# Attention over neighbours, then order statistics of neighbours: the search for neighbours in seven blocks instead of six, and seven edits to what waits for what

## The chip, the cores and the metric

The kernel runs on one core of a Trainium2 chip. The metric is the device time of the whole program in microseconds (us), the median over several runs; lower is better. The engines are named as in the profile: PE (matrix), PEld (its weight loads), DVE (vector), ACT (scalar), POOL (general, here the issuer of indirect DMAs) and SP (here the issuer of plain DMAs).

## What is computed

Inputs are 4096 nodes of 128 features and a 4096 x 4096 adjacency matrix of integers, some 64 neighbours in a row and at most 100. Layer 0 is graph attention with eight heads, layer 1 takes quantiles over neighbours. Cut to what matters:

```python
# layer 0
Wh = einsum('nd,hde->hne', nodes, W)
e = leaky_relu(f1[:, :, None] + f2[:, None, :], 0.2)       # f1, f2 from Wh, a1, a2
att = softmax(where(adj > 0, e, -9e15), axis=-1)
h = elu(einsum('hnm,hmd->hnd', att, Wh))
x = layernorm(nodes + elu(cat_of_heads(h) @ W1 + b1)) * gamma + beta
# layer 1
rank = cumsum(adj != 0, axis=1) - 1
keep = mask & ~((rank + 1) % skip == 0)                    # skip: about half the count of neighbours
svals = sort(where(keep, x, big), axis=neighbours)         # each feature by itself
agg = sum over q in (0.25, 0.5, 0.75) of svals[ceil(q * n_keep) - 1] / 3
out = (0.5 * agg + 0.5 * x) @ W.T + b + x
```

## The kernel before

The kernel is written for a framework that records instructions in program order and then orders each engine's queue itself: among the instructions that its own timing model holds ready it takes the one recorded first. The order on an engine is thus fixed when the program is built, by that model's times. `tc.issue_after(ins)` keeps what is recorded inside it behind `ins` on the same engine; `tc.declare_no_dep(a, b)` takes away a dependency that the framework would otherwise keep by a semaphore.

**Search.** The nodes are 32 tiles of 128 rows. `Front` finds each row's neighbours: SP loads the adjacency in quarters of a tile (L378), ACT turns them to 0 and 1 (L380, L387), PE packs 16 columns into a word (L389), and DVE draws the non-empty words and then the columns out of the words by rounds of eight maxima (`first`, `second` and a last drain, L188 and L190). Tiles are grouped into blocks, `BLOCKS = (4, 4, 6, 6, 6, 6)`, and inside a block the rows are ordered by their count of neighbours: `place` computes each row's place (`pos_i`, L518), and POOL writes its list there by an indirect DMA (L541 into `rows_d`). Since the rows are ordered, each group of 16 rows has a bound on its count of neighbours that holds for any likely input; `BOUNDS[n]` lists it for a block of n tiles, and a flag sends other inputs to a general path. `keep` writes what layer 1 needs (`meta_d`), and at the end `order` computes each row's place among all 4096 rows, which 32 indirect DMAs write into `order_d` (L680, `late` in `gat`).

`Front.pieces` cuts this work into a list: for each block, one `first` per tile, a `second` for up to four tiles together, a last drain per tile, `place`, and `keep` of the block before. `gat` draws from the list: `EARLY` = 5 pieces ahead of the loop, two after each half tile (`advance(2)`), and `through(b)` until block b is placed where its lists are needed.

**Attention.** `gat` goes over 64 half tiles u, each 64 rows. `load(u)` has POOL gather the neighbours' rows of `xf_d` (L971, 128 rows by one DMA, into buffers `nb`) and, once a tile, the tile's own rows (`me`, L947); it runs three half tiles ahead. Ahead of a block's first gathers SP loads the lists back (L903, L919, L932). `probabilities` has DVE and ACT form the logits and the softmax (L1054 to L1088), starting from `mine` (L989), which needs `me`; `rows_sum` spreads the weights over rows (DVE, L1103) and PE sums the products (L1111). `combine` takes two tiles at a time, in stages drawn one per half tile from the list `going`, through the heads' matrices and the layer norm (to L1194), and POOL writes the rows to their nodes' places in `x1_d` (L1197, in the profile `x_d<-s`).

**Sort.** `sparse` goes over 32 tiles of the globally ordered rows. `load(t)` has POOL gather the tile's `info` (L1867), its own rows `xs`, and 50 to 100 neighbours a row (L1713) from `x1_d` into one of three buffers `rows`. A network of comparators then sorts the neighbours of all 128 rows and 128 features at once. A step compares up to 16 pairs of columns: ACT copies the lower ones aside (L1751), to one of two PSUM tiles `low` or, up to four pairs, to SBUF (`low_s`), and DVE writes minimum (L1756) and maximum (L1757). `plan` splits a tile's network into a first part and the final merge; the second part of tile t-1 and the first part of tile t are interleaved. The steps of tile 0's first part take 8 pairs instead of 16. `quantile` and `pick` find the quantiles: ACT scales the candidates by weights of zero or one (L1810), PE sums them (L1815, L1818), and every four tiles `finish` applies the last layer on PE (L1835 to L1837), which ACT copies out (L1841) and POOL stores (L1845). This work waits in a list, `waiting`, and is put between the comparator's instructions: each step draws at most one entry, and PE's products go to the last 512 columns of a PSUM tile whose first columns a step of at most 12 pairs uses.

The sort begins with its own loads of `order` and a count `iota_p`, inside the branch that is taken once the flag has been read.

Of the kernel before, what the change touches and what calls it, by code (L numbers as in the profile page):

```python
# [50 lines left out]
P = 128  # L51
# [19 lines left out]
C3 = 8  # L71
# [21 lines left out]
MOST = 16  # L93
# [4 lines left out]
BLOCKS = (4, 4, 6, 6, 6, 6)  # L98
# [13 lines left out]
BOUNDS = {  # L112
    4: (
# [203 lines left out]

class Front:
# [88 lines left out]
    def second(self, t, m, k1, cand):  # L407

        nc, one = self.nc, self.one
        k1, cand = k1[:, :m], cand[:, :m]  # L410
        sp = self.spill[:, t : t + m, :]
        wf, base = decode(nc, one, k1, f"1_{m}")
        rest = one.tile([P, m, C1], F32, name=f"rest1_{m}")
        peel(nc, one, wf, base, cand[:, :, :C1], rest, f"1_{m}")
# [5 lines left out]
        k2 = one.tile([P, m, C2], F32, name=f"k2_{m}")  # L420
# [5 lines left out]
        wf, base = decode(nc, one, k2, f"2_{m}")  # L426
        rest = one.tile([P, m, C2], F32, name=f"rest2_{m}")
        peel(nc, one, wf, base, cand[:, :, C1 : C1 + C2], rest, f"2_{m}")
        nc.vector.tensor_scalar(base, base, 127.0 * NG1, None, op0=ALU.add)
        nc.vector.scalar_tensor_tensor(rest, rest, float(NG1), base, op0=ALU.mult, op1=ALU.add)  # L430
        k3 = one.tile([P, m, C3], F32, name=f"k3_{m}")
# [5 lines left out]
        wf, base = decode(nc, one, k3, f"3_{m}")  # L437
        for r in range(PEELS):
            nxt = one.tile([P, m, C3], F32, name=f"rest3_{m}", bufs=2)
            at = C1 + C2 + C3 * r  # L440
            peel(nc, one, wf, base, cand[:, :, at : at + C3], nxt, f"3_{m}")
            wf = nxt
        left = one.tile([P, m], F32, name=f"left_{m}")
# [353 lines left out]
def gat(tc, nc, c, x, adj, xf_d, meta_d, order_d, flag_d, w, a1, a2, w1, b1, gamma, beta, x1_d):  # L797
# [25 lines left out]
    with ExitStack() as ctx:  # L823
# [307 lines left out]
        def combine(t, zT):  # L1131
# [64 lines left out]
            for j in range(TWO):  # L1196
                nc.gpsimd.indirect_dma_start(  # L1197
# [4 lines left out]
                )  # L1202

        held = {u: load(u) for u in range(3)}
# [5 lines left out]
        for u in range(2 * NT):  # L1210
# [3 lines left out]
            elif late:  # L1214

                advance(len(todo))
                for piece in late:
                    piece()
                late = []
# [3 lines left out]
            if u + 1 < 2 * NT:  # L1223
                with ExitStack() as order:
                    for ins in behind:
                        order.enter_context(tc.issue_after(ins))
                    e, behind = probabilities(u + 1, held[u + 1], f1s[(u + 1) // 2])
            with ExitStack() as order:
                for ins in behind:
                    order.enter_context(tc.issue_after(ins))  # L1230
# [7 lines left out]
            advance(2)  # L1238
        for stages in going:
            for _ in stages:  # L1240
                pass
        advance(len(todo))
# [415 lines left out]
def plan(t):  # L1658
# [8 lines left out]
    first = steps(layers[:-merge], lambda i: i, PAIRS if t else PAIRS // 2)  # L1667
# [7 lines left out]
def sparse(tc, nc, c, x1_d, meta_d, order_d, w, b, out):  # L1675


    with tc.tile_pool(name="sp1", bufs=1) as one, tc.tile_pool(
# [15 lines left out]
        it = one.tile([P, 2 * MIDDLE], I32, name="it_p")  # L1694
# [612 lines left out]
```

## Time and profile before

| | |
|---|---|
| median of 3 runs | 8430.65 us (8417.16 to 8433.30) |
| profiled execution | 7646.96 us, of which the span is 7645.2 us |
| busy in the span | DVE 5831.7, POOL 4343.5, ACT 2214.1, PE 1122.8, PEld 946.8 us |
| gathers of the attention (L971) | 2190, 953 ns each, from 142.5 to 3106.6 us |
| gathers of the sort (L1713 `rows`) | 2078, 971 ns each, from 3170.6 to 7265.4 us |
| comparators (L1756, L1757, large steps) | 1022 each, 1862 and 1861 ns |
| POOL waiting for rows buffers (`rows` on ACT `picked`) | 1270.8 us in 28 waits |
| DVE waiting for gathers (L1054 on `nb`) | 1206.7 us in 115 waits |

The profiled execution is one of its own and took less time than the runs of the median, so a sum made from the profile is compared with the profiled time. A group of instructions has its busy time, its mean and the idle time of its engine just before it, with what ended that idle time. In a timeline a row gives start and length, the instruction, and in brackets the idle time before it and its releaser.

### The profile page before, as it was taken

Reading aid. Unit: us, or ns where it says so; the run is one execution under the profiler, and the core shown is the slowest. Engines: PE = TensorE matmul, PEld = TensorE weight load, DVE = VectorE, ACT = ScalarE, POOL = GpSimd, SP = SyncE. Lnnn points to the kernel's source line nnn. Section 1 sums busy time; section 2 is a strip of 40 time slices with the busy share of each in tenths; the row PEclk is TensorE's granted clock in tenths of the full one; section 3 lists DMA queues with packets and bytes.
Section 4 is the critical chain, followed back from the end, with each engine's and each line's share of the span. In section 5 each row is a group of like instructions: output and inputs, shape, how many; then the busy total and the mean of one; then the engine's idle time right before and its main releaser. Section 6 shows DMA issues by size and latency. Waiting matters only on the chain. (4 is left out here: it accounts for less than half of the span.)

```text
span 7645.2 us, 31290 instructions
## 1 busy us (share of the span) xinstructions
PE 1122.8 (15%) x6047; PEld 946.8 (12%) x6047; DVE 5831.7 (76%) x9380; ACT 2214.1 (29%) x2301; POOL 4343.5 (57%) x4524
## 2 busy tenths in 40 slices
PE   3243333322222322100000000000000000000001
PEld 1232222222222222100000000000000000000000
DVE  8465555565223222399999999999999999999999
ACT  6020212100000000144344343434334433443433
POOL 2777677777777777565554645455536434554500
PEclk5566666666566666655555555555555555555555
DMA  6242324222222222111111111111101101111100
GB/s 205 57 121 56 107 62 121 60 55 56 47 56 56 56 56 56 40 44 34 40 35 30 41 31 37 30 36 34 38 23 41 34 24 33 36 35 29 33 1 1
DMA packets 219057, 380.95 MB, mean 50 GB/s; under 512 B 129283, under 2 KB 129412, under 8 KB 218852
## 3 DMA queue, kind: packets, MB, share of 16 engines
q0 software_dynamic: 145808, 308.58, 15.3%
q1 hardware_dynamic: 72898, 70.23, 3.1%
q14 instruction: 156, 1.28, 0.1%
q8 instruction: 49, 0.80, 0.0%
q10 hardware_dynamic: 146, 0.07, 0.0%
HBM read 368.26 MB, written 10.31 MB: 50 GB/s over the span
## 5 line engine op out<-in xcount | busy, mean ns | idle before, releaser
L1713 POOL DMA_INDIRECT rows<-x_d,info x2078 | 2018.2, 971 | 1949.5 <-ACT picked L1810 1270.8
L971 POOL DMA_INDIRECT nb<-xf_d,ids x2190 | 2086.0, 953 | 707.0 <-issue 632.2
L1751 ACT COPY low<-rows 128x2048 f32<-128x2048 f32 (+8 forms) x1022 | 1561.5, 1533 | 2429.9 <-DVE rows L1757 1780.7
L1756 DVE TENSOR_TENSOR rows<-low,rows 128x2048 f32<-128x2048 f32 (+9 forms) x1022 | 1884.7, 1862 | 138.9 <-ACT low L1751 50.0
L1757 DVE TENSOR_TENSOR rows<-low,rows 128x2048 f32<-128x2048 f32 (+9 forms) x1022 | 1882.4, 1861 | 5.8
L1054 DVE TENSOR_TENSOR e<-nb,ps_small 128x64 f32<-128x64 f32 (+9 forms) x200 | 47.7, 240 | 1252.6 <-DMA nb<-xf_d,ids 1206.7
L1111 PE MATMUL ps_z<-spread,nb 128*128 128x128 f32 x4500 | 615.7, 305 | 797.9 <-DVE spread L1103 775.6
L1111 PEld LDWEIGHTS ps_z<-spread,nb 128*128 128x128 f32 x4500 | 604.5, 220 | 829.9 <-DVE spread L1103 420.7
L1815 PE MATMUL low<-sixth_i,picked 128*128 128x128 f32 x300 | 79.8, 442 | 4224.7 <-ACT low L1751 3736.4
L1815 PEld LDWEIGHTS low<-sixth_i,picked 128*128 128x128 f32 x300 | 66.8, 324 | 4237.7 <-ACT low L1751 3744.8
L1073 ACT ACTIVATE ps_e<-e 128x256 f32<-128x256 f32 (+4 forms) x64 | 26.1, 408 | 1936.2 <-DVE e L1054 972.6
L1103 DVE TENSOR_TENSOR spread<-e,ps_small 128x1152 f32<-128x1152 f32 (+4 forms) x312 | 342.7, 1107 | 129.2 <-PE ps_z L1111 79.4
L1845 POOL DMA_INDIRECT out<-o,info x32 | 34.4, 1076 | 392.9 <-ACT o L1841 369.2
L380 ACT ACTIVATE nz<-a_i 128x1024 bf16<-128x1024 int32 x128 | 134.3, 1051 | 292.5 <-DMA a_i<-in_adj 254.3
L1751 ACT COPY low_s<-rows 128x512 f32<-128x512 f32 (+3 forms) x325 | 139.8, 471 | 130.5 <-DVE rows L1756 48.0
L389 PE MATMUL ps_words<-nz,pows 128*128 128x512 bf16 (+1 forms) x272 | 113.7, 577 | 364.4 <-ACT nz L387 258.0
L188 DVE MAX8 k<-key 128x8 f32<-128x256 f32 x416 | 164.6, 412 | 0.7
L1756 DVE TENSOR_TENSOR rows<-low_s,rows 128x512 f32<-128x512 f32 (+3 forms) x325 | 158.3, 500 | 3.0 <-ACT low_s L1751 2.1
L1757 DVE TENSOR_TENSOR rows<-low_s,rows 128x512 f32<-128x512 f32 (+3 forms) x325 | 158.7, 500 | 0.3
L190 DVE MATCH_REPLACE8 key<-k,key 128x256 f32<-128x256 f32 x384 | 155.5, 407 | 0.0
L1142 PE MATMUL ps_h<-zT,w_ga 128*128 128x256 f32 x256 | 116.3, 619 | 198.4 <-DVE s L1414 106.6
L1759 DVE TENSOR_TENSOR rows<-rows 128x256 f32<-128x256 f32 (+8 forms) x245 | 141.6, 580 | 0.2
(246 smaller groups left out, 2528.0 us busy)
## 6 DMA issues: line engine op xcount, KB each, us to landing
a_i<-in_adj SPq DMA_DIRECT2D x128, 512.0 KB
nb<-xf_d,ids POOLq DMA_INDIRECT x2190, 2.5
rows<-x_d,info POOLq DMA_INDIRECT x2078, 2.5
xf_d<-xf POOLq DMA_DIRECT2D x4, 576.0 KB, 7.4
xf<-in_x POOLq DMA_DIRECT2D x4, 512.0 KB
meta_d<-rowdata_k SPq DMA_DIRECT2D x4, 324.0 KB
abc_ta<-in_L_gnn_a POOLq DMA_DIRECT2D x2, 512.0 KB, 7.7
w_ga<-in_L_gnn_W POOLq DMA_DIRECT2D x2, 512.0 KB
```

Source lines behind the costliest of these rows:

```text
L188: nc.vector.max(out=top, in_=work)
L190: nc.vector.match_replace(out=work, in_to_replace=top, in_values=work, imm_value=gone)
L380: nc.scalar.activation(nz[:, j, :], a_i, AF.Relu, scale=-1.0, accum_out=self.negative[:, k : k + 1],)
L971: gather = nc.gpsimd.indirect_dma_start(out=rows[:, used + i, :], out_offset=None, in_=xf_d, in_offset=bass.IndirectOffsetOnAxis(ap=ids[:, ...
L1103: last = nc.vector.tensor_tensor(spread[:, :m], e[:, at : at + m, :].unsqueeze(2).to_broadcast(shape), own.unsqueeze(1).unsqueeze(3).to_br ...
L1111: product = nc.tensor.matmul(ps_z[:, g, :], rows[:, k, :D], spread[:, i].rearrange("p j h -> p (j h)"), start=i0 + i == 0, stop=i0 + i == ...
L1713: nc.gpsimd.indirect_dma_start(out=row, out_offset=None, in_=x1_d, in_offset=bass.IndirectOffsetOnAxis(ap=info[:, col : col + 1], axis=0),)
L1751: nc.scalar.copy(packed, lows)
L1756: nc.vector.tensor_tensor(lows, packed, highs, op=ALU.min)
L1757: nc.vector.tensor_tensor(highs, packed, highs, op=ALU.max)
L1759: nc.vector.tensor_tensor(lows, lows, highs, op=ALU.min)
L1815: nc.tensor.matmul(made["ps"], made["v"][:, i, :], sixth, start=i == 0, stop=False)
```

## The change

The blocks become 2, 4, 4, 6, 6, 6 and 4 tiles, with a table of bounds for two tiles, and in the first 20 half tiles three pieces of the search are drawn instead of two. To this come the edits of what waits for what:

- the stores into `x1_d` no longer depend on each other;
- the 32 writes of the order are kept behind the last half tile's gathers on POOL;
- `order` and the `info` of tiles 0 and 1 are loaded in `gat`, ahead of the last `combine`, and `iota_p` is made at the start;
- minimum and maximum of a step no longer depend on products in other columns of the PSUM tile;
- the scalings of a pick are drawn one at a time;
- a tile's own rows are gathered after its neighbours, and a tile's `info` and gathers are kept behind the gathers of the tile before;
- tile 0's first part takes steps of 4 pairs.

The temporary tiles of `second` are shared between counts of tiles (names without the count, all of `BATCH` size), and `picked` holds 14 rows instead of 16. Cut to these, the diff is:

```diff
-MOST = 16
+MOST = 14
-BLOCKS = (4, 4, 6, 6, 6, 6)
+BLOCKS = (2, 4, 4, 6, 6, 6, 4)
 BOUNDS = {
+    2: (54, 58, 58, 60, 62, 62, 64, 66, 66, 68, 70, 70, 72, 76, 78, 100),
...
+class Batches:
+    def __init__(self, pool):
+        self.pool = pool
+    def tile(self, shape, dtype, name, **kw):
+        full = [shape[0], BATCH, *shape[2:]]
+        return self.pool.tile(full, dtype, name=name, **kw)[:, : shape[1]]
...
     def second(self, t, m, k1, cand):
-        nc, one = self.nc, self.one
+        nc, one = self.nc, Batches(self.one)
...
 def gat(...):
             for j in range(TWO):
-                nc.gpsimd.indirect_dma_start(
+                done = nc.gpsimd.indirect_dma_start(
                     out=x1_d,
...
+                for other in stored:
+                    tc.declare_no_dep(done.ins, other, reason="each node has a row of its own")
+                stored.append(done.ins)
...
                 advance(len(todo))
-                for piece in late:
-                    piece()
+                with tc.issue_after(gathers[2 * NT - 1][HALF - 1, 0]):
+                    for piece in late:
+                        piece()
...
-            advance(2)
-        for stages in going:
+            advance(3 if u < 2 * START[3] else 2)
+        for stages in going[:-1]:
             for _ in stages:
                 pass
-        advance(len(todo))
+        for i in range(4):
+            nc.sync.dma_start(
+                out=order[:, ts(i, NT // 4)],
+                in_=order_d[ts(i, N // 4), :].rearrange("(t p) c -> p (t c)", p=P),
+            )
+        for t, info in enumerate(infos):
+            nc.gpsimd.indirect_dma_start(
+                out=info,
+                out_offset=None,
+                in_=meta_d,
+                in_offset=bass.IndirectOffsetOnAxis(ap=order[:, t : t + 1], axis=0),
+            )
+        for stages in going[-1:]:
+            for _ in stages:
+                pass
...
 def plan(t):
-    first = steps(layers[:-merge], lambda i: i, PAIRS if t else PAIRS // 2)
+    first = steps(layers[:-merge], lambda i: i, PAIRS if t else PAIRS // 4)
...
 def compare(rows, step):
                 nc.scalar.copy(packed, lows)
+                aside = []
                 if waiting and waiting[0][0] == "copy":
                     waiting.pop(0)[1]()
                 elif waiting and SMALL < k <= PAIRS - FOUR:
-                    waiting.pop(0)[1](t[:, (PAIRS - FOUR) * D :])
-                nc.vector.tensor_tensor(lows, packed, highs, op=ALU.min)
-                nc.vector.tensor_tensor(highs, packed, highs, op=ALU.max)
+                    aside = waiting.pop(0)[1](t[:, (PAIRS - FOUR) * D :])
+                for to, op in ((lows, ALU.min), (highs, ALU.max)):
+                    done = nc.vector.tensor_tensor(to, packed, highs, op=op)
+                    for product in aside:
+                        tc.declare_no_dep(done.ins, product, reason="other columns of the bank")
...
 def pick(found, x1, comT):
-            def scale():
-                made["v"] = tp.tile([P, MOST, D], F32, name="picked", bufs=1)
-                for i, (v, weight) in enumerate(found):
-                    nc.scalar.mul(made["v"][:, i, :], v, weight)
+            def scale(i):
+                if i == 0:
+                    made["v"] = tp.tile([P, MOST, D], F32, name="picked", bufs=1)
+                nc.scalar.mul(made["v"][:, i, :], *found[i])
...
-            return [
-                ("copy", scale),
+            return [("copy", lambda i=i: scale(i)) for i in range(len(found))] + [
                 ("bank", sums),
...
 def load(t):
-            info = three.tile([P, MW], I32, name="info", bufs=3 * FOUR)
-            group[first][2].append(info)
-            nc.gpsimd.indirect_dma_start(
-                out=info,
-                out_offset=None,
-                in_=meta_d,
-                in_offset=bass.IndirectOffsetOnAxis(ap=order[:, t : t + 1], axis=0),
-            )
-            gather(group[first][0][:, t - first, :], info, NODE)
-            for s in range(HIGH[t]):
-                gather(rows[:, s, :], info, s)
+            with ExitStack() as after:
+                if gathered:
+                    after.enter_context(tc.issue_after(gathered[-1]))
+                if t < len(infos):
+                    info = infos[t]
+                else:
+                    info = three.tile([P, MW], I32, name="info", bufs=2 * FOUR + 2)
+                    nc.gpsimd.indirect_dma_start(
+                        out=info,
+                        out_offset=None,
+                        in_=meta_d,
+                        in_offset=bass.IndirectOffsetOnAxis(ap=order[:, t : t + 1], axis=0),
+                    )
+                group[first][2].append(info)
+                for s in range(HIGH[t]):
+                    done = gather(rows[:, s, :], info, s)
+                gather(group[first][0][:, t - first, :], info, NODE)
+                gathered.append(done.ins)
```

## The prediction

> **What bounds the kernel now.** I read the busy slices first, then windows, then the timeline of single engines at the places where one stage hands over to the next. The page's slices show two stages with different limits:
>
> ```profile
> PE   3243333322222322100000000000000000000001
> ...
> DVE  8465555565223222399999999999999999999999
> ...
> POOL 2777677777777777565554645455536434554500
> ```
>
> A slice is 191 us. Up to slice 17 POOL is the steady engine (the attention layer); from there DVE stands at 9 (the sorting layer). Two windows (sums for PE, PEld, DVE, ACT, POOL, then clock and DMA) say the same in numbers:
>
> ```profile
> 2400.00:2600.00 200.00, 45.23 (x277) 41.91 (x276) 51.15 (x136) 11.44 (x21) 150.82 (x160) 0.60 0.24 56
> ...
> 4500.00:5500.00 1000.00, 35.33 (x126) 28.79 (x126) 967.43 (x628) 396.11 (x303) 533.86 (x540) 0.50 0.12 35
> ```
>
> In the first, 160 indirect DMAs in 200 us are 1.25 us each: 0.95 of work and 0.30 of "issue" before each. POOL is full, though it shows 75%. In the second DVE is idle 33 us in 1000. So the attention layer ends when POOL's queue is empty, and the sort when DVE's is. POOL's timeline at the start (start, length, instruction, idle before and its releaser):
>
> ```profile
> 133.25 1.04 POOL L541 DMA_INDIRECT rows_d<-rowdata,pos_i  x1 [57.96 <-DVE pos_i L518]
> ...
> 142.51 0.99 POOL L971 DMA_INDIRECT nb<-xf_d,ids  x1 [4.40 <-DMA ids<-rows_d]
> ```
>
> POOL waits 58 us for DVE to find and place the neighbours of the first block, and the first gather goes out at 142.5. From there to 3106.6 POOL runs 2314 instructions, about 2900 us at 1.253, and waits about 64. Among them, by the view of the tile, are the order's writes:
>
> ```profile
> L680 POOL DMA_INDIRECT order_d<-node,pos_g x32: 954/958/991, 1920.5 to 2026.1; - x32
> ```
>
> They sit between gathers, in the middle of the full queue. At its end POOL stands still:
>
> ```profile
> 3105.62 0.94 POOL L971 DMA_INDIRECT nb<-xf_d,ids  x1 [0.30 <-issue]
> 3146.65 0.98 POOL L1197 DMA_INDIRECT x_d<-s,info  x1 [40.09 <-DVE s L1194]
> ...
> 3162.97 0.99 POOL L1867 DMA_INDIRECT info<-meta_d,order  x1 [0.72 <-issue]
> ...
> 3170.57 0.94 POOL L1713 DMA_INDIRECT rows<-x_d,info  x1 [0.30 <-issue]
> ```
>
> It idles 40 us for the last layer norms, and the sort's first row is fetched 64 us after the last gather. In the sort, DVE's waits from 3240 us on (total, times, longest):
>
> ```profile
> DVE rows L1756 <- ACT low L1751: 46.5, 48, 1.9
> DVE rows L1756 <- PE low L1837: 20.3, 8, 3.3
> DVE rows L1756 <- PE low L1818: 12.3, 10, 2.2
> ```
>
> DVE waits 33 us for matmuls whose products it does not read. Their surroundings, once:
>
> ```profile
> 5761.84 2.29 DVE L1756 TENSOR_TENSOR rows<-low,rows 128x2048 f32<-128x2048 f32 x1 [1.94 <-ACT low L1751]
> 5766.58 1.23 DVE L1756 TENSOR_TENSOR rows<-low,rows 128x1024 f32<-128x1024 f32 x1 [2.45 <-PE low L1837]
> ```
>
> [...] 128x768 takes 0.96 us and 128x1024 1.22, which leaves 0.18 at no columns.
>
> **The change part by part**, against the profiled 7645.2 us.
>
> *Two tiles first.* The maxima of tiles 0 and 1 are done at 45.1 us in DVE's timeline; for four tiles `second` ran 79.8 to 95.1 (15), the last drains to 123 (7.0 a tile), `place` to 133 (10). For two I take 11, 14 and 9: 79 us. The pad memsets, which waited until 70.6, may hold DVE on the way: plus 4. From `pos_i` to the first gather it was 9.6 us with four scatters, 7 with two. First gather at 90: **-52** (-45 to -60). The counts of the two bound tables give 2196 gathers instead of 2190: +7.5. Two more of the 32 neighbour scatters fall after the first gather: +2.5.
>
> *Does the second block come in time?* Its gathers are due after 141 gathers and two `me`, 179 us after the first: at 269. Before, DVE was held at `mine` of tile 1 until 77 us after the first gather, since that row comes in turn. Now that is near 171; behind it stand four drains (28), `place` (10) and two half tiles' logits and spreads (22): 231, then 10 to the gathers. It is in time by 28 us, and POOL still pays the landing chain that cost 4.4 at the first block: +5 (0 to 80, the upper end if `place` stands behind half tile 3's logits on DVE). The three later stalls on `info<-rows_d`, 12.3 us in five block edges, become six edges: +2.5.
>
> *Three pieces of search per half tile.* DVE spent 942 us in 200 to 1800, and 287 per 1000 where no search runs (2000 to 3000). A half tile's attention costs 0.287 x 44.9 = 13 us; what remains of the search is 582 us by my count for 30 tiles and 83 pieces, 7 a piece. Two pieces make 27 us, three 34, against 44.9 of gathers. Gathers cover it: 0. The cover is buffers for about two half tiles ahead; its failures cost 36.9 before (POOL on `ps_z`).
>
> *Order written last.* 32 x 1.256 = **-40.2** in the full queue. They now lie in the 40.09 us of idle after the last gather and end just when the first `x_d` store is ready: covered, to within 2 us. *Stores without waits for each other:* -10.6 in the queue (POOL on `x_d<-s`).
>
> Sum to the last gather: -52 + 7.5 + 2.5 + 5 + 2.5 - 40.2 - 10.6 = **-85**.
>
> *Hand-over.* Behind the last order write (+41 us after the last gather) SP loads the order (landing 3.6, four loads, 2 to land: +49), then POOL the two infos and the last two stores (ready at +48.3 as before): +54, landed +56.5. Rows start at +57 instead of +64: **-7** (-10 to +3, if SP's loads land late, since the last stores queue behind them). The iota and the `xs` gather leave the way too; they are in this number.
>
> *Finer steps for tile 0.* Between 3170.6 and 3236 DVE worked 21 us of 65. With 4-pair steps the first starts 10 us earlier and more fits; some 25 more steps cost 2 x 0.18 each, 9 us, in idle time. The next tile's rows arrive no earlier: **-6** (-12 to +5).
>
> *Products not waited for.* The 12.3 of L1818 go, less 1. The 20.3 of L1837 come with waits of 1.7 to 1.9 on ACT just before, five of them, because the matmul held the smaller step back (second line above): 29.7 together. But the products take 6 us, and the bank's next copy stands behind the copy of the products; I keep 13. Together **-24** (0 to -40).
>
> *Scaling one at a time.* The 46.5 us on ACT are mostly copies that start the moment DVE ends, data or bank, not bursts of scaling: 0 (-5 to +5). Rows buffers come free four steps later, some 13 us; POOL waited 15 us or more for all but one of them, and tile 31's landed about 30 us before its use. *Infos behind the gathers:* 2.4 us per tile in that same slack. The shared tiles and MOST change no instruction on a queue.
>
> Total -85 - 7 - 6 - 24 = **-122**: 7523 span, 7525 with the 1.8 around it. The median of the runs shown is 1.1025 times the profiled 7647.0; I see no reason in the profile and scale all: 8430.65 x 7525/7647 = **8296**.
>
> **Rivals.** *B, the gather queue starves:* the second block comes 50 us late or the denser search holds back the buffers. For it: 21.6 us at 883 and 8.5 at 820 already, with DVE at 66%. Against it: all 28 later scatters waited only for issue. The 52 are lost: -70, 8353. *C, new waits:* the bank's release takes the products' place and the order's loads land late: -31 gone, -91, 8330. *D, slower:* DVE becomes the bound of the first 20 half tiles. It decides from 122/20 = 6 us over the 44.9 a half tile, 51 against my 34; at 56 us it costs 220: +98, 8539. Against it: 17 us of room. *E, the order's writes do not move,* or land on the last stores' way: -82, 8340.
>
> **Chances.** All parts: 0.58, its own range 8245 to 8340. B 0.18, C 0.08, E 0.06, D 0.07, about level 0.03. Only D is slower; 0.2% is about what a measurement of this kernel can tell from no change. The best ends together give -160 (8254), and 8235 if gathers count for more outside the profile; the high end takes B and some of its excess. Range 8235 to 8375.
>
> **What would show it.** First gather near 90 and no POOL idle over 10 us near 270; L680 after the last L971; last gather near 3021; rows 57 us after it; no DVE wait on L1818 or L1837, and a small one on ACT in place of the latter. Wrong if POOL shows more than 100 us on `ps_z` or `pos_i`, or if DVE's idle time in the sort stays above 75 us.

## The result and the profile after

The changed kernel took 8584.31 us (median of 4 runs, 8568.83 to 8590.3), the kernel before beside it 8431.97 (8417.16 to 8437.66): ratio **1.0181, interval 1.0162 to 1.0199**. It is 152 us slower where 135 us less were forecast; 8584 lies far above the range.

The sign goes with the chip: on two chips (called here the **7650 chips**) the kernel before takes 7648 to 7651 us, on two others (the **8400 chips**) 8381 to 8426. One of the 8400 chips was used twice, more than two hours apart, with the 7650 chips in between, and gave 8426 and 8421; each other chip was used once. By its 7645 us the profile of before that the prediction read belongs to the first kind; the runs above, before and after, belong by their times to the second. On a 7650 chip the same changed kernel is faster, 7558.88 against 7647.76: ratio **0.9883, interval 0.9867 to 0.9900**.

The busy slices of the changed kernel as recorded, 215 us each:

```profile
PE   2213222223232323230000000000000000000000
...
DVE  4646466554222222234898979989899898998999
...
POOL 4454555566666666657255435536454535444410
```

Where POOL stood at 7 in the profile of before it stands at 4 to 6, and DVE in the sort drops from an even 9 to 8 in many slices. In windows (sums for PE, PEld, DVE, ACT, POOL, then clock and DMA):

```profile
2400.00:2600.00 200.00, 53.70 (x251) 46.04 (x250) 45.61 (x120) 9.44 (x18) 136.61 (x145) 0.58 0.20 51
...
4500.00:5500.00 1000.00, 35.32 (x126) 28.79 (x126) 921.59 (x691) 377.09 (x311) 481.56 (x503) 0.50 0.12 33
```

POOL issues 145 DMAs in the first window against 160, and DVE idles 78 us in the second against 33. Neither queue is full. The times of single steps, by POOL's timeline (start, length, instruction, idle before and its releaser), at the first block:

```profile
93.20 1.04 POOL L553 DMA_INDIRECT rows_d<-rowdata,pos_i  x1 [16.32 <-DVE pos_i L530]
...
101.30 0.98 POOL L985 DMA_INDIRECT nb<-xf_d,ids  x1 [5.75 <-DMA ids<-rows_d]
```

and at the hand-over to the sort:

```profile
3758.20 0.94 POOL L985 DMA_INDIRECT nb<-xf_d,ids  x1 [0.30 <-issue]
3759.45 0.99 POOL L692 DMA_INDIRECT order_d<-node,pos_g  x1 [0.30 <-issue]
...
3798.64 0.96 POOL L692 DMA_INDIRECT order_d<-node,pos_g  x1 [0.30 <-issue]
...
3833.09 0.99 POOL L1211 DMA_INDIRECT x_d<-s,info  x1 [24.84 <-DVE s L1208]
...
3845.67 0.98 POOL L1736 DMA_INDIRECT rows<-x_d,info  x1 [2.17 <-ACT sixth_i L1726]
```

Each part of the change is where the diff puts it. The first gather is 41 us earlier; the order's writes lie behind the last gather. But the last layer norms, ready 40 us after the last gather in the profile of before, are ready 74 us after it. DVE's waits in the sort, from 3930 us on (total, times, longest):

```profile
DVE rows L1781 <- ACT low L1774: 183.8, 30, 44.9
DVE rows L1781 <- issue: 93.6, 30, 33.1
DVE rows L1781 <- remote: 31.2, 14, 3.2
```

The waits on products are gone, as meant, and far more has come on ACT and under "issue" and "remote". A semaphore is, in the records of the trace, what one engine or DMA moves when it is done and another waits for; this trace holds 23,529 such movements. "Remote" means that the semaphore moved and neither an instruction that ended in the 1.5 us before nor a DMA in the profile goes with it; "issue", that no wait is seen at all.

### The profile page after: what moved, and what is told of

Its sections match the earlier page's. It is cut to its first block, busy times and chain, and to the rows that moved or that the text cites. A ratio compares the mean times of both kernels' runs of the same rounds, so it can differ in the third digit from the quotient of the medians.

```text
span 8584.5 us, 31606 instructions
## 1 busy us (share of the span) xinstructions
PE 1246.5 (15%) x6061; PEld 1041.6 (12%) x6061; DVE 5894.7 (69%) x9558; ACT 2221.1 (26%) x2340; POOL 4339.1 (51%) x4530
## 5 line engine op out<-in xcount | busy, mean ns | idle before, releaser
L1781 DVE TENSOR_TENSOR rows<-low,rows 128x2048 f32<-128x2048 f32 (+10 forms) x1970 | 3650.9, 1893 | 269.4 <-ACT low L1774 183.8
L1774 ACT COPY low<-rows 128x2048 f32<-128x2048 f32 (+8 forms) x985 | 1528.4, 1557 | 2310.6 <-DVE rows L1781 1711.5
L1125 PE MATMUL ps_z<-spread,nb 128*128 128x128 f32 x4512 | 759.9, 325 | 1363.8 <-issue 766.5
L1117 DVE TENSOR_TENSOR spread<-e,ps_small 128x640 f32<-128x640 f32 (+4 forms) x314 | 342.9, 1105 | 812.6 <-remote 648.8
L1125 PEld LDWEIGHTS ps_z<-spread,nb 128*128 128x128 f32 x4512 | 704.7, 237 | 1443.0 <-issue 944.3
L1781 DVE TENSOR_TENSOR rows<-low_s,rows 128x512 f32<-128x512 f32 (+3 forms) x798 | 395.1, 523 | 127.8 <-remote 36.5
L1774 ACT COPY low_s<-rows 128x512 f32<-128x512 f32 (+3 forms) x399 | 179.6, 486 | 289.4 <-DVE rows L1781 175.4
L1140 ACT COPY zT<-ps_z 128x512 f32<-128x512 f32 x64 | 37.6, 587 | 707.8 <-remote 520.6
L1068 DVE TENSOR_TENSOR e<-nb,ps_small 128x56 f32<-128x56 f32 (+9 forms) x202 | 45.2, 237 | 178.3 <-DMA nb<-xf_d,ids 153.3
L189 DVE MAX8 lists<-cand 128x8 f32<-128x176 f32 x416 | 127.1, 329 | 44.5 <-remote 26.5
```

The source lines that it names most:

```text
L189: nc.vector.max(out=top, in_=work)
L1117: last = nc.vector.tensor_tensor(spread[:, :m], e[:, at : at + m, :].unsqueeze(2).to_broadcast(shape), own.unsqueeze(1).unsqueeze(3).to_br ...
L1125: product = nc.tensor.matmul(ps_z[:, g, :], rows[:, k, :D], spread[:, i].rearrange("p j h -> p (j h)"), start=i0 + i == 0, stop=i0 + i == ...
L1774: nc.scalar.copy(packed, lows)
L1781: done = nc.vector.tensor_tensor(to, packed, highs, op=op)
```

## The experiments

**A copy of the kernel before**, on an 8400 chip.

> The kernel before, unchanged, for a profile beside its own runs. Theory 1 (the 7645 us profile that the prediction was built on is not how the kernel runs: each engine stalls for reasons that profile does not show): a span near 8430 us, POOL waiting several hundred us on PE's ps_z in the attention, DVE idle 200 us or more in the sort. Theory 2 (that profile is typical, and only the changed kernel stalls): a span near 7645 us and POOL waiting under 100 us in the attention.

Measured: 8424.5 beside 8425.63 (0.9998, 0.9988 to 1.0008), profiled span 8422.6. The 7645 us of the first profile are not how this chip runs the kernel. In the lines below the lengths of the instructions hardly differ; the idle time between them does. The softmax of one half tile in DVE's timeline, first in the profile the prediction was made from:

```profile
2529.64 0.49 DVE L1039 TENSOR_REDUCE most<-ps_e 128x32 f32<-128x320 f32 x1
2530.17 0.21 DVE L1007 STREAM_TRANSPOSE most_t<-most 128x32 f32<-128x32 f32 x1
2530.41 0.19 DVE L1011 TENSOR_REDUCE most_b<-most_t 128x4 f32<-128x32 f32 x1
2530.63 0.18 DVE L1014 COPY most_t<-most_b 128x32 f32<-128x32 f32 x1
```

and the like sequence in the copy on the 8400 chip:

```profile
2501.96 0.19 DVE L1011 TENSOR_REDUCE den_b<-den_t 128x4 f32<-128x32 f32 x1 [1.20 <-DVE den_t L1007]
2503.35 0.18 DVE L1013 RECIPROCAL den_b<-den_b 128x4 f32<-128x4 f32 x1 [1.21 <-issue]
2504.76 0.24 DVE L1014 COPY den_t<-den_b 128x32 f32<-128x32 f32 x1 [1.23 <-issue]
2506.15 0.21 DVE L1016 STREAM_TRANSPOSE den_r<-den_t 128x32 f32<-128x32 f32 x1 [1.16 <-DVE den_t L1014]
```

Instructions of 0.2 us that follow each other start every 0.22 us there and every 1.40 us here. In the sort the copy has a long wait that the first profile does not have at all, above one that it has too (46.5 us there; DVE, from 3930 us on):

```profile
DVE rows L1756 <- remote: 191.4, 8, 42.2
DVE rows L1756 <- ACT low L1751: 38.9, 35, 2.4
```

The two traces of this one kernel also differ in a way that the page does not show. The first profile has no "remote" wait on any engine; the copy has 299. In 52 of DVE's (812 us of idle time) and 36 of ACT's (720 us) the semaphore is PE's, in 157 of DVE's (383 us) it is DVE's own. In the median these engines start 0.02 us after the semaphore moves, but the last instruction to move it had ended long before: in the median 15 us for DVE's waits on PE, 2.3 us for DVE's waits on itself. So it is the message that comes late, not the work. In the same stretches records of such movements are missing: of all semaphore movements, those of landing DMAs among them, the first profile holds 87,013 and the copy 24,217. In the first 142 us, up to the first gather, they have 1545 and 1526; from 300 to 1000 us, under the gathers, 11,211 and 2291. All eleven traces from the 8400 chips hold 23 to 25 thousand, all nine from the 7650 chips 87 to 88 thousand.

**The parts of the change in two heaps**, on the same chip. First the changed kernel with the six blocks and two pieces of before, so with the edits to waits alone (tile 0's finer steps are counted among them):

```diff
-BLOCKS = (2, 4, 4, 6, 6, 6, 4)
+BLOCKS = (4, 4, 6, 6, 6, 6)
...
-            advance(3 if u < 2 * START[3] else 2)
+            advance(2)
```

> The seven edits of waits alone, with the six blocks of before and two pieces a half tile. Theory 1 (the blocks and the denser search cost the time, the edits of waits save some 40 to 80 us): ratio to before 0.990 to 0.996. Theory 2 (the edits of waits cost it, since the order's writes now stand after the last gather and the attention is not bound by POOL's queue): ratio 1.01 to 1.02.

Measured: 8469.87, ratio 1.0057 (1.0038 to 1.0075). A miss for both theories: the waits do cost, but a third of the loss. Then the other heap, the kernel before with the seven blocks, the shared tiles and three pieces, and none of the edits to waits:

```diff
-BLOCKS = (4, 4, 6, 6, 6, 6)
+BLOCKS = (2, 4, 4, 6, 6, 6, 4)
...
-            advance(2)
+            advance(3 if u < 2 * START[3] else 2)
```

> The seven blocks and the three pieces a half tile alone, none of the edits of waits. Theory 1 (the blocks and the denser search cost the time): ratio 1.02 to 1.03, POOL waiting more on ps_z in the first 1300 us than before. Theory 2 (the edits of waits cost it): ratio 0.995 to 1.003.

Measured: 8533.64, 1.0118 (1.0094 to 1.0142), the larger part. And the changed kernel with two pieces, its blocks kept:

```diff
-            advance(3 if u < 2 * START[3] else 2)
+            advance(2)
```

> The whole change, with two pieces of search a half tile as before. If the pace of the search is the cost, ratio 1.00 or below; if the two-tile block or the edits of waits are, ratio stays at 1.015 to 1.02.

Measured: 8526.25, 1.0113 (1.0090 to 1.0135), which falls between: within the change the pace is worth some 0.7%. In that kernel the last gather ends 62 us later than in the one with the waits alone (3701.9 against 3640.1).

**Parts taken back or done alone, on a 7650 chip** (before: 7651.12). Tile 0's steps of 8 pairs put back into the changed kernel:

```diff
-    first = steps(layers[:-merge], lambda i: i, PAIRS if t else PAIRS // 4)
+    first = steps(layers[:-merge], lambda i: i, PAIRS if t else PAIRS // 2)
```

> The changed kernel with tile 0's sort steps of up to half a bank again (8 pairs), as before. Theory 1: the 4-pair steps are what lengthened the sort, since each step is a hand-over between DVE and ACT that takes place while POOL's queue is full of row gathers, and hand-overs then come late; tile 4's rows, which came 71 us later than in the kernel before (397 against 326 us after the first row), are back near 326, the sort ends 80 to 95 us earlier, ratio to before 1.006 to 1.009. Theory 2, the prediction's: the finer steps lie in idle time and gain 6 us; ratio 1.018 to 1.020 and the sort as long as now.

Measured: 7563.8, ratio 0.9888 (0.9872 to 0.9905). Neither: the kernel gained 87 us here. Three pieces alone in the kernel before:

```diff
-            advance(2)
+            advance(3 if u < 20 else 2)
```

> The kernel before, its six blocks kept, with three pieces of search per half tile in the first 20 half tiles. Theory 1: the denser search alone makes the attention longer, because DVE's instructions of the search come slowly while POOL gathers: gather 700 comes 80 to 130 us later than in the copy of before (1301), part of it comes back when the search ends earlier, and the end is 40 to 60 us later, ratio 1.005 to 1.007. Theory 2: the pace hurts only together with blocks of two tiles: ratio 0.998 to 1.001. The prediction's step (27 us of DVE against 44.9 becomes 34) gives 1.000.

Measured: 7631.92, 0.9974 (0.9964 to 0.9984): on this chip the pace gains a little. Spare writes in the kernel before, which nothing waits for:

```diff
+                        if t == 0:
+                            self.spare_writes(to)
...
                 for piece in late:
                     piece()
                 late = []
+                front.scatters = []
+                with tc.issue_after(gathers[2 * NT - 1][HALF - 1, 0]):
+                    for i in range(NT):
+                        front.scatter(i, front.pos_g, front.last_d)
```

> The kernel before with writes that nothing waits for, into tensors of their own: 16 of 4 bytes per partition behind the drain of tile 0, while POOL waits for the first neighbours, and 32 more behind the last gather, where the changed kernel has the order's. The drains and the last layer norms are untouched. Theory 1, POOL's issuing holds up the other engines: drains of tiles 1 to 3 and the place step, 38 us from the first drain to pos_i in the copy of before, take 6 us or more longer, and the first store of the last four comes 70 to 76 us after the last gather in place of 40. Theory 2, the writes lie beside other work as the prediction has it: both within 2 us of the copy (38, and 40 to 43 us).

Measured: one time of 7660.46; from the first drain to `pos_i` 38.0 us, from the last gather to the first of the last four stores 41.0. The writes are covered, as theory 2 says. Last, the changed kernel with blocks, pace, tile 0's steps and the place of the order's writes as before:

```diff
-BLOCKS = (2, 4, 4, 6, 6, 6, 4)
+BLOCKS = (4, 4, 6, 6, 6, 6)
...
-                with tc.issue_after(gathers[2 * NT - 1][HALF - 1, 0]):
-                    for piece in late:
-                        piece()
+                for piece in late:
+                    piece()
...
-            advance(3 if u < 2 * START[3] else 2)
+            advance(2)
...
-    first = steps(layers[:-merge], lambda i: i, PAIRS if t else PAIRS // 4)
+    first = steps(layers[:-merge], lambda i: i, PAIRS if t else PAIRS // 2)
```

> The changed kernel with what seems to cost taken back: the six blocks and two pieces of before, tile 0's steps of 8 pairs, the order's writes where the planner puts them. What stays: products not waited for, stores without waits for each other, scaling one at a time, the order and two lists loaded ahead, lists behind the gathers. Theory 1: these gain some 40 us in the steady sort (from tile 5's rows to the end 4091 us in the kernel with all seven waits, 4133 in the copy of before), the hand-over stays near 64: ratio 0.993 to 0.997. Theory 2: the gain of the sort comes from the finer steps of tile 0 only shifting work, and nothing is left: 0.999 to 1.002.

Measured: 7591.59, 0.9922 (0.9905 to 0.9939): the remaining edits gain 60 us here.

**The same on the other 7650 chip** (before: 7647.76), with the changed kernel itself.

> The changed kernel once more. The kernel before has so far taken about 7650 us in one session and about 8430 in two, with the same instructions of the same lengths, and in the second case with idle time behind DVE, ACT and PE instructions that no wait of the profile explains. Theory 1: the sign of the change hangs on that condition. Beside a before of 8430: 1.018 again. Beside a before of 7650: the sum of the prediction is nearly right for all but tile 0's finer steps; with their expected gain of 6 us 0.988, with a loss of 50 us 0.995. Theory 2: the change is slower in both: 1.01 or more beside either.

Measured: 7558.88, 0.9883 (0.9867 to 0.9900). The sign depends on the chip.

> The changed kernel with tile 0's sort steps of 8 pairs, as before. Beside a before of 7650 it took 0.989. Theory 1: beside a before of 8430 it is slower than before, since the denser search under POOL's gathers and the order's writes ahead of the last layer norms still cost there; the finer steps take 80 to 95 us of the 153 that were lost, 1.006 to 1.009. Theory 2: 4-pair steps are all that was wrong and the rest gains as beside 7650: 0.99.

Measured: 7562.67, 0.9888 (0.9871 to 0.9904), so that the finer steps are worth 4 us on this chip. The spare writes and the kernel with most taken back came out as before:

> The kernel before with 16 spare writes behind the drain of tile 0 and 32 behind the last gather, that nothing waits for. Beside a before of 7650 the step from the first drain to pos_i and the first of the last four stores were as without them (41 us behind the last gather against 40). Theory 1: beside a before of 8430, POOL's issuing holds up the others: from the first drain to pos_i 6 us or more longer than 38, the first store 70 to 76 us behind the last gather. Theory 2, POOL's issuing is not what holds them up: 38 and 40 to 43 there too.

Measured: 7654.31 once, 40.8 us from the last gather to the store; from the first drain to `pos_i` 41.3.

> The changed kernel with blocks, pace, tile 0's steps and the order's writes as before; the other waits stay away. Beside a before of 7650 it took 0.992. Theory 1: its gains (products, stores, lists ahead) are waits that are gone in either condition, so beside a before of 8430 it is the only form that is faster: 0.993 to 0.997. Theory 2: there the waits are hidden behind other idle time: 0.999 to 1.002.

Measured: 7591.35, 0.9926 (0.9910 to 0.9943).

**The same on an 8400 chip** (before: 8381.35; the copy of before above ran on the other one). The spare writes first:

> The kernel before with 16 spare writes behind the drain of tile 0 and 32 behind the last gather, that nothing waits for. Beside a before of 7650: nothing moves (40 to 43 us from the last gather to the first of the last four stores, as twice measured). Beside a before of 8430, theory 1, POOL's issuing holds up the others: from the first drain to pos_i 6 us or more longer than 38, the first store 70 to 76 us behind the last gather. Theory 2, something else holds them up: 38 and 40 to 43 there too.

Measured: 8417.26 once. The first of the last four stores comes **69.9 us** after the last gather, against 40.4 in the copy without the writes: theory 1. This is the hand-over in the timelines of ACT, DVE and POOL:

```profile
3692.63 0.47 ACT L1181 ACTIVATE yT<-ps_h,b_ga 128x256 f32<-128x256 f32 x1 [28.78 <-remote]
...
3694.07 2.42 DVE L1121 TENSOR_TENSOR spread<-e,ps_small 128x640 f32<-128x640 f32 x3 [27.90 <-remote]
```

```profile
3684.95 0.96 POOL L693 DMA_INDIRECT last_d<-node,pos_g  x1 [0.31 <-issue]
3715.28 0.96 POOL L1215 DMA_INDIRECT x_d<-s,info  x1 [29.37 <-DVE s L1212]
```

and the same two instructions of the same kernel on the 7650 chip:

```profile
3132.04 0.47 ACT L1181 ACTIVATE yT<-ps_h,b_ga 128x256 f32<-128x256 f32 x1 [6.65 <-PE ps_h L1178]
...
3132.70 0.82 DVE L1121 TENSOR_TENSOR spread<-e,ps_small 128x640 f32<-128x640 f32 x1 [4.46 <-PE ps_z L1129]
```

Nothing but the chip differs. While POOL issues writes that concern nobody, ACT and DVE stand 28 us, and they go on 6.7 and 8.2 us after POOL's last write (3685.9). Without the writes the chain from the last gather to the store takes 40.4 us on the 8400 chip and 40.1 in the first profile: with POOL silent the chips are alike. The other half of the test is a miss for theory 1: drain to `pos_i` took 40.2 us, inside what the 7650 chips showed (38.0 and 41.3), although 16 spare writes went out under the drains. A run of DVE instructions among themselves was not held up there. But the condition of the gathers had not set in either: over these writes and 5 us more this trace holds 391 semaphore movements, those of the 7650 chips 457 and 450, while from 150 to 230 us, under the first gathers, it holds 133 against 1510 on the first 7650 chip. So this half of the test was made ahead of the stalls and speaks neither for nor against theory 1.

The changed kernel with tile 0's steps of 8 pairs:

> The changed kernel with tile 0's sort steps of 8 pairs. Beside a before of 7650: 0.989, as twice measured. Beside a before of 8430, theory 1: 1.006 to 1.009, the finer steps being 80 to 95 us of the loss of 153; theory 2: 0.99, the finer steps being all of it.

Measured: 8474.03, 1.0114 (1.0097 to 1.0131): slower without the finer steps too, by a little more than expected.

And the version with most taken back:

> The changed kernel with blocks, pace, tile 0's steps and the order's writes as before, the other waits gone. Beside a before of 7650: 0.992, as twice measured. Beside a before of 8430, theory 1: 0.993 to 0.997, since these waits are gone in either condition; theory 2: 0.999 to 1.002.

Measured: 8362.7, 0.9976 (0.9968 to 0.9984): a gain, half of what theory 1 gave it. Of the versions run on both kinds of chip it is the only one that is faster than before on both; on a 7650 chip the changed kernel gains more.

**Single parts alone in the kernel before, on an 8400 chip** (before: 8421.06). The order's writes behind the last gather:

```diff
-                for piece in late:
-                    piece()
+                with tc.issue_after(gathers[2 * NT - 1][HALF - 1, 0]):
+                    for piece in late:
+                        piece()
```

> The kernel before with the order's 32 writes behind the last gather, and nothing else. Theory 1, POOL's stream holds the other engines up in one condition and not in the other: beside a before of 7650 the prediction's step is right, 40 us less, 0.994 to 0.996; beside a before of 8400 the gathers end 40 us earlier but the first of the last four stores comes 70 to 76 us behind them in place of 40, so that 5 to 15 us are left: 0.998 to 1.000. Theory 2, the writes are covered in both: 0.995 in both.

Measured: 8412.22, 0.9990 (0.9983 to 0.9997), as theory 1 has it. The last gather ends at 3637.1 against 3679.1 in the copy, 42 us earlier, and the first of the last four stores comes 70.6 us later in place of 40.4. What POOL's queue saves, the layer norms lose. Next, tile 0's steps of 4 pairs:

```diff
-    first = steps(layers[:-merge], lambda i: i, PAIRS if t else PAIRS // 2)
+    first = steps(layers[:-merge], lambda i: i, PAIRS if t else PAIRS // 4)
```

> The kernel before with tile 0's sort steps of 4 pairs in place of 8, and nothing else. Theory 1: beside a before of 7650 a few us (the changed kernel with and without them: 0.9883 and 0.9888), 0.999 to 1.000; beside a before of 8400 each step's hand-over between ACT and DVE comes late while POOL gathers the rows of tiles 0 to 3, and 55 to 85 us are lost, 1.006 to 1.010. Theory 2, the steps gain 6 us in either: 0.999.

Measured: 8494.29, 1.0086 (1.0069 to 1.0103), as theory 1 has it. DVE's waits in the first 515 us of this kernel's sort:

```profile
DVE rows L1757 <- remote: 36.1, 17, 3.2
DVE rows L1757 <- issue: 33.6, 20, 3.0
...
DVE rows L1757 <- DVE rows L1757: 13.3, 17, 1.4
```

Many small gaps of 1 to 3 us, where the copy has 6.9 of "remote" and 2.7 of "issue" ahead of L1757 up to the same point of the work, its first 435 us. All gaps ahead of L1757 together are 88 us here and 13 there, which is the 73 us that the kernel lost. In each of them the semaphore is DVE's own: it is the hand-over from the minimum to the maximum on the same engine that comes late, and not the one from ACT to DVE that theory 1 named. Tile 4's rows are all fetched 505 us after the first row, in the copy 431. Last the three pieces, with the edit shown above:

> The kernel before with three pieces of search in the first 20 half tiles, and nothing else. Beside a before of 7650 it took 0.997. Theory 1: beside a before of 8400 the search holds the half tiles back, since DVE's steps come late under the gathers; in the changed kernel the pace made 0.7% there; 1.004 to 1.008. Theory 2: it is the two-tile block that makes the pace hurt; alone 0.997 to 1.001.

Measured: 8532.18, **1.0128** (1.0111 to 1.0144): theory 1's sign, and more than it gave. The pace alone costs 111 us, as much as blocks and pace together (1.0118). The windows from 300 to 1000 us, first three pieces on the 8400 chip, then on the 7650 chip:

```profile
300.00:1000.00 700.00, 175.29 (x870) 139.13 (x870) 361.21 (x1563) 113.52 (x179) 372.77 (x392) 0.59 0.28 73
```

```profile
300.00:1000.00 700.00, 237.76 (x1276) 188.93 (x1276) 513.26 (x2290) 186.39 (x290) 506.03 (x528) 0.64 0.42 108
```

In the same 700 us DVE gets through 1563 instructions against 2290, and POOL through 392 DMAs against 528. POOL's waits in these stretches, again 8400 first:

```profile
POOL nb L971 <- PE ps_z L1111: 204.1, 9, 58.6
```

```profile
POOL nb L971 <- PE ps_z L1111: 28.5, 5, 24.4
```

DVE is busy 52% of the window and POOL still waits for it, through PE: the half tile's chain of hand-overs is what is slow, not the amount of DVE's work. No run here shows which of these hand-overs weighs most.

## Why the prediction was wrong, point by point

From the profiled executions, in us; "before, 8400" is the copy, and "changed, 7650" the changed kernel on the second 7650 chip. The first gather lies within the time to the last:

| | before, 7650 | changed, 7650 | difference | before, 8400 | changed, 8400 | difference |
|---|---|---|---|---|---|---|
| first gather | 142.5 | 100.9 | -41.6 | 142.3 | 101.3 | -41.0 |
| end of last gather | 3106.6 | 3073.5 | -33.0 | 3679.1 | 3759.1 | +80.0 |
| from there to the first row | 64.0 | 57.7 | -6.4 | 63.9 | 86.5 | +22.6 |
| first row to the end | 4474.6 | 4425.5 | -49.1 | 4679.6 | 4738.8 | +59.2 |
| sum of the last three | 7645.2 | 7556.7 | -88.5 | 8422.6 | 8584.5 | +161.9 |

The forecast sums were -85, -7 and -30, together -122. On the 7650 chip -88.5 is not far off, but in part by luck: the attention gained 52 us less than forecast and the sort 19 us more.

**The step that failed first** is the last: "The median of the runs shown is 1.1025 times the profiled 7647.0; I see no reason in the profile and scale all". A tenth between a profile and its runs is not a factor on every duration. The runs came from the other kind of chip, whose extra time is idle time in the chains between engines, as the lines of the softmax show. The premises read from the profile, POOL full in the attention and DVE full in the sort, hold on the one kind only. On the 8400 chip POOL waits 663 us in the attention of the kernel before, by the sum of its waits over 0.35 us, and 67 in the first profile. Both of the prediction's own signs of being wrong came in the changed kernel there: POOL waits 497 us on `ps_z` (78 on the 7650 chip), and DVE idles 336 us in the sort from 3930 us on (38 on the 7650 chip, from 3210 us on). The terms below that changed sign are those that lie under POOL's stream.

**Three pieces: "Gathers cover it: 0".** Gathers 100 to 1000 are 26.3 half tiles. One of them takes 47.5 us in the first profile and 48.8 with three pieces on a 7650 chip, so there the cover held. On the 8400 chip it takes 58.2 with two pieces and 66.0 with three. Alone the pace costs 111 us; that is rival D, in sign, in place and nearly in its price (8 us per half tile against the 11 it assumed). Its mechanism was only half right: half tiles are bound through DVE's hand-overs, with DVE 52% busy, and not by the amount of its work.

**The head start.** The first gather at 101 instead of 90 is 10 us short of the step. On the 8400 chip the other 41 are gone by gather 200, at 460 us in the changed kernel and 458 in the copy. Of the +80 at the last gather, the sum of POOL's waits explains most: they rise by 161 (663 to 824), more gathers and two moved scatters by 10 (the prediction's count), against 41 from the head start and 40 from the order's writes. That makes +90. Blocks and pace do not add: to the last gather the blocks at two pieces cost 62 us (in the kernel with the edits to waits), the pace on six blocks 116, both together 112.

On the 7650 chip -33 came in place of -85: 10 from the first gather (no run takes that apart), and 42 from POOL's waits, which rose by 39 (67 to 106) where the prediction had them fall by 3. Two places hold it. At the second block POOL waits 17.0 us in place of the 5 that I gave. And once it stops outright:

```profile
693.64 0.94 POOL L985 DMA_INDIRECT nb<-xf_d,ids  x1 [47.23 <-PE ps_z L1125]
```

DVE had stood 25.0 us at `mine` until 644.3, for a row of `me` that comes in turn behind POOL's gathers, and then worked off drains of the search that stood ahead of the half tile's spreads. The prediction had seen this hold-up at the second block and not asked for it at a later one. That is a piece of rival B.

**Order's writes: "covered, to within 2 us".** On the 7650 chip it is so: the first of the last four stores is 50.7 us after the last gather, behind the two lists as the step has it, and the sort starts at 57.7 (57 forecast). On the 8400 chip the cover is no cover: the engines that should work under the writes stand still. The kernel with this part alone gives the price, 42 us gained and 30 lost.

**Finer steps for tile 0: -6 (-12 to +5).** On the 7650 chip -4 (7558.88 against 7562.67). On the 8400 chip +73 alone (8494.29 against 8421.06), and some 55 within the change (1.0181 against 1.0114, from two groups of runs). The step priced only the 0.18 us that each instruction has beyond its columns, an estimate from 0.96 us of DVE at 128x768 and 1.22 us at 128x1024; the hand-over from minimum to maximum that goes with each had no price. On the 8400 chip it comes up to 3.2 us late in 59 of the 184 pairs (10 of 145 in the copy).

**Products not waited for: -24, scaling: 0.** Better than forecast on the 7650 chip. With tile 4's rows fetched, the sort stood 6 us ahead; at the end 49. DVE's waits on the products (32.6) are gone and those on ACT fell from 46.5 to 35.0. That minimum and maximum can run beside products into other columns of their PSUM tile was an assumption of the prediction; the profile of before does not show it. The changed kernel's trace on the 8400 chip does: the products of the second group of four tiles run from 5028.0 to 5035.9, and the minimum and maximum of the step that shares their tile (128x896) start at 5029.12 and 5030.24 and take 1.09 us each, the mean of all 40 of that shape.

On the 8400 chips the step's own doubt, that the tile's next copy stands behind the copy of the products, becomes the larger part. Every four tiles ACT copies out the last layer's products (L1877 in the changed kernel). ACT's line for the second of these groups, first on the 8400 chip, then on the 7650 chip:

```profile
5078.24 0.58 ACT L1877 COPY o<-low 128x512 f32<-128x512 f32 x1 [47.42 <-remote]
```

```profile
4182.83 0.59 ACT L1877 COPY o<-low 128x512 f32<-128x512 f32 x1 [5.09 <-PE low L1869]
```

PE's last product had ended at 5035.9 and at 4182.8: 42 us before the copy in the one case, nothing in the other. The same is so for all of the first seven groups: 19 to 42 us against at most 0.4. In the kernel before, DVE's minimum waits for that product itself, which makes up most of the 191.4 us of "remote" in the copy. The edit takes DVE's wait away, but ACT's next copies stand in its queue behind the copy-out (the first at 5078.85, right after the one above), and DVE waits for them (44.95 us, until 5080.54). Seven such stops hold 196 of the 246 us that DVE idles after tile 4's rows are fetched, in the copy 187 of 279. The sort of the version with most taken back is 17 us shorter (4659.2 from the first row to the end; 4676.1 in the kernel with the spare writes on the same chip).

What stays open is why these chips differ. The instructions are the same, the granted clock is alike (0.551 and 0.547 for the kernel before), and single durations agree (128x2048 minima and maxima: 2.28 us in the first profile and in the changed kernel on an 8400 chip). Shown is that a longer stream of POOL's indirect DMAs is enough to lengthen the stall at the hand-over (69.9 us from the last gather to the store against 40.4). That the stream is behind every gap in attention and sort is argued, from the runs with the finer steps and with the denser search and from the records that go missing once the gathers begin, not shown; no run here took the gathers away. One rival is untested. Each run on record has a span from the profiler, and on the 8400 chips most of the semaphore movements are missing (24,217 recorded for the kernel before, against 87,013). It may be that the movements themselves are held up on these chips, or that recording them is what holds them up; no run here tells which, nor how the two kinds of chip compare when nothing is recorded.

## What to carry to other kernels

If a profile and its timed runs differ by a tenth, do not scale: take the profile again, compare idle times before instructions and the number of semaphore movements recorded, and find the excess before any stage is called full. Call a stage full only if its engine's waits are near zero in an execution that lasts as long as the timed ones (POOL's in the attention: 67 us in the first profile, 663 in the copy). And price a hand-over between engines as well as the instruction: smaller steps gained 4 us on a 7650 chip and lost 73 on an 8400 chip, and the layer norms laid "beside" the order's writes came 30 us later on an 8400 chip, so keep first the edits that only take waits away, as those of the version that was faster on both. And when a wait is taken from one engine, look who else waits for the same event and stands ahead of it.

## What the runs showed of the hardware that was not expected

- One program, with single instructions of the same lengths, takes 7648 to 7651 us on two chips and 8381 to 8426 on two others.
- On the slower kind, 32 indirect writes of POOL that no other engine depends on go with a stop of ACT and DVE, which wait for PE's semaphore, of 28 us; they go on 7 to 8 us after the last one. On the other kind the same writes cost at most 1 us there.
- There, in the copy of before, 299 waits ended more than 1.5 us after the last instruction that moves their semaphore had ended, in the first profile none; and 24,217 semaphore movements are recorded in place of 87,013.
- There a copy of ACT that waits for PE's last product of a group starts 19 to 42 us after that product has ended, on the other kind at most 0.4 us after it (changed kernel, first seven groups).
- There DVE instructions of 0.2 us that depend on each other were seen to start every 1.40 us in place of 0.22.
